# A Mamba layer and a window attention layer on four images: one pipeline over all images per layer, in place of both layers image by image

## The chip, the cores and the metric

The kernel runs on one core of one Trainium2 chip. The metric is the time of one execution in microseconds (us), measured on the device. The engines are PE (matmuls), DVE (VectorE), ACT (ScalarE), POOL (GpSimd) and SP, whose queue issues the DMA transfers.

## The reference, cut to what matters

The input x is 4 images of 384 channels and 64 x 64 points, in fp32. Two layers follow, each with a residual, each on x normalised in groups of 12 channels over a whole image. (The residuals and group norms are not in this cut. `bn_stats`, below, is the DVE instruction that gathers means and variances for them.)

```python
# layer 0, a state space layer: 768 inner channels, 16 states, 4096 points in sequence
xn = layernorm(xs) * ln_w + ln_b
xb, z = split(xn @ in_proj_w.T)
xc = silu(causal_conv4(xb) + conv_b)
dt, Bm, Cm = split(xc @ x_proj_w.T)            # 24 + 16 + 16
dt = softplus(dt @ dt_w.T + dt_b)
h  = exp(dt * A) * h + (dt * xc) * Bm          # point after point
y  = (sum over states of h * Cm) + xc * D
out = (y * silu(z)) @ out_proj_w.T
# layer 1: attention with 12 heads, each point with a 7 x 7 window and a relative bias
```

The group norm is why a layer can't start on an image before it has seen the whole image: its statistics come first.

## The kernel before: the parts that matter here

The sequence of one image is cut into 16 steps of 256 points. For each of 6 channel blocks and each of 4 groups of states, ACT makes `da = exp(dt*A)`, POOL makes `db = dtx*B`, DVE runs four scans (`hp` and `hs`, two each), DVE and POOL multiply by C, and PE adds up the states and turns the result. That is one unit; a step has 24 units and 48 slots, two for each unit. All other work of a step (projections, convolution, a burst of Silu with its table loads, softplus, normalisation, output projection) is put by hand into numbered slots between the scans:

```python
def scan(d, g, h, db, y, ahead):
    ...
    for half, to in ((0, hp), (1, hs)):
        da = ps_a.tile([P, 2, T], F32, tag="da", name="da")       # 2 PSUM banks
        ... # two exponentials on ACT, two scans on DVE
        ahead()                                                   # emits the work of the next slot
# work of a step, by slot
at(26, by_group); at(27, lambda: mean("xn", "mu")); ...           # normalisation of the step after next
pair(("c", p), 9 + 3 * p, ...); at(12 + 3 * p, conv_out)          # convolution on PE, copied out by ACT
at(27, burst)                                                     # six Silu between two table loads
softplus(q, 31 + 3 * q)                                           # q = 0, 1, 2
# output projection of the step before: three tiles on PE, residual on DVE
at(8, lambda: tiles(0, (0,)));  at(9, lambda: tiles(0, (1,)))
at(10, lambda: residual(0, 2))
at(11, lambda: tiles(2, (2,))); at(12, lambda: residual(2, 1))
```

(The calls of `at` are drawn together here.) Most matmul results pass through one pool of three banks of PSUM, the memory into which PE writes. The frame around it handles one image after the other:

```python
bm = ...                           # mask, then 96 small transfers of the relative bias
for b in range(NB):
    ...                            # load x, bn_stats for the group norm
    layer0(b, x1, lambda pool: group_stats(st0, pool, f"a{b}"), st1)
    layer1(b, x1, lambda pool: group_stats(st1, pool, f"b{b}"))
```

## Time and profile before

| | before |
|---|---|
| time | 9843.51 us, median of 3 runs (9839.28 to 9846.54) |
| span of the profiled execution | 9830.4 us |
| step of the state space layer | 104.86 us |
| start, up to the first exponential | 179.4 us |

The page's busy line and three of its rows in 40 slices (a digit is the busy share in tenths):

```profile
PE 7857.1 (80%) x46266; PEld 5693.4 (58%) x46266; DVE 7503.0 (76%) x15348; ACT 5802.9 (59%) x13694; POOL 6099.0 (62%) x5279
...
PE   4787787799777777779968778777997778777899
DVE  3888888655688888865568888885556888888555
...
POOL 2898899400399898830049889893005889889200
```

POOL's row shows the four images: it is busy in the state space layer and idle in attention.

### The profile page before, as it was taken

How to read it: one execution, taken by the hardware profiler on the slowest of the kernel's cores; microseconds unless marked ns; L12 is line 12 of the kernel's file. 1: busy time of each engine (PE TensorE's matmuls, PEld its weight loads, DVE VectorE, ACT ScalarE, POOL GpSimd, SP SyncE). 2: the span in 40 equal slices, each digit the busy share in tenths (PEclk: the TensorE clock that was granted, in tenths of full speed). 3: DMA queues.
4: the chain of work that ended last, by engine and by line, in shares of the span. 5: the costliest groups of instructions: out<-in, count | busy, mean ns of one | idle time of the engine just before them, and what ended most of it. 6: DMA issues, size and time to landing. Idle time of an engine off the chain costs nothing. (4 is left out here: it accounts for less than half of the span.)

```text
span 9830.4 us, 139829 instructions
## 1 busy us (share of the span) xinstructions
PE 7857.1 (80%) x46266; PEld 5693.4 (58%) x46266; DVE 7503.0 (76%) x15348; ACT 5802.9 (59%) x13694; POOL 6099.0 (62%) x5279
## 2 busy tenths in 40 slices
PE   4787787799777777779968778777997778777899
PEld 4666666455566666645556666664555666666455
DVE  3888888655688888865568888885556888888555
ACT  3667667344566666634456766763445766766344
POOL 2898899400399898830049889893005889889200
PEclk9788888799888888789988888888998888887899
DMA  2111111222211111112221111112222111111222
GB/s 82 56 48 42 57 47 40 69 74 68 70 52 45 50 50 45 53 59 77 70 73 45 42 58 45 44 55 71 75 61 72 42 57 47 42 59 42 73 75 61
DMA packets 300170, 563.61 MB, mean 57 GB/s; under 512 B 61196, under 2 KB 183324, under 8 KB 298804
## 3 DMA queue, kind: packets, MB, share of 16 engines
q1 hardware_dynamic: 299444, 554.67, 17.5%
q8 instruction: 365, 5.98, 0.3%
q14 instruction: 361, 2.96, 0.1%
HBM read 452.01 MB, written 84.73 MB: 55 GB/s over the span
## 5 line engine op out<-in xcount | busy, mean ns | idle before, releaser
L96 ACT ACTIVATE da<-dt,nega 128x256 f32<-128x256 f32 x6144 | 2914.2, 477 | 1628.7 <-DVE hs L501 1085.7
L481 POOL TENSOR_TENSOR db<-dtx,B 128x1024 f32<-128x1024 f32 x1536 | 3614.0, 2353 | 30.2
L501 DVE TENSOR_TENSOR_SCAN hp<-da,state,db 128x256 f32<-128x256 f32 x3072 | 2298.6, 748 | 429.5 <-POOL dtx L476 216.2
L501 DVE TENSOR_TENSOR_SCAN hs<-da,state,db 128x256 f32<-128x256 f32 x3072 | 2255.3, 734 | 18.3 <-ACT da L96 15.2
L520 PE MATMUL y<-ident,hv 128*128 128x128 f32 x6144 | 1206.6, 330 | 1145.7 <-DVE hv L507 1144.6
L512 POOL TENSOR_TENSOR hs<-hs,C 128x512 f32<-128x512 f32 x1536 | 1946.5, 1267 | 123.2 <-POOL state L511 0.6
L520 PEld LDWEIGHTS y<-ident,hv 128*128 128x128 f32 x6144 | 859.9, 168 | 1571.6 <-DVE hv L507 1464.6
L96 ACT ACTIVATE sg<-sg,mx 128x308 f32<-128x308 f32 x1536 | 830.3, 542 | 884.0 <-DVE mx L798 883.0
L851 POOL COPY rb<-rsum 128x384 f32<-128x384 f32 x128 | 65.8, 514 | 2052.9 <-DVE rsum L849 1935.2
L520 PE MATMUL y<-ident,hs 128*128 128x128 f32 x6144 | 1165.4, 323 | 141.5 <-POOL hs L512 139.2
L330 PE MATMUL mm_ps<-xn,w_in 128*128 128x256 f32 x4608 | 1118.3, 390 | 14.6 <-DVE xn L306 8.1
L507 DVE TENSOR_TENSOR hv<-hp,C 128x512 f32<-128x512 f32 x1536 | 1043.3, 679 | 0.0
L520 PEld LDWEIGHTS y<-ident,hs 128*128 128x128 f32 x6144 | 899.9, 170 | 206.8 <-POOL hs L512 202.4
L330 PEld LDWEIGHTS mm_ps<-xn,w_in 128*128 128x128 f32 x4608 | 874.9, 198 | 126.4 <-issue 9.9
L798 DVE CUSTOM_DVE_ANT_0 sg<-lg_ps,bias 128x308 f32<-128x308 f32 x1536 | 650.9, 474 | 237.4 <-PE lg_ps L792 226.6
L337 PE MATMUL mm_ps<-xb,dcv 128*128 128x256 f32 x3072 | 723.4, 379 | 0.0
L337 PEld LDWEIGHTS mm_ps<-xb,dcv 128*128 128x128 f32 x3072 | 562.8, 190 | 68.7
L511 POOL COPY state<-hs 128x2 f32<-128x2 f32 x1536 | 286.4, 186 | 500.6 <-DVE hs L501 456.3
L476 POOL TENSOR_TENSOR dtx<-dt,xc 128x256 f32<-128x256 f32 x384 | 279.3, 727 | 465.7 <-DMA B<-bcrows 297.2
L556 PE MATMUL mm_ps<-yg,w_out 128*128 128x256 f32 x2304 | 523.6, 382 | 0.0
L822 DVE COPY ta<-pt_ps 110x512 f32<-110x512 f32 x768 | 495.1, 680 | 25.0 <-PE pt_ps L817 21.7
L556 PEld LDWEIGHTS mm_ps<-yg,w_out 128*128 128x128 f32 x2304 | 437.4, 192 | 57.8
(136 smaller groups left out, 10438.8 us busy)
## 6 DMA issues: line engine op xcount, KB each, us to landing
B<-bcrows SPq DMA_DIRECT2D x256, 512.0 KB
C<-bcrows SPq DMA_DIRECT2D x256, 512.0 KB
vw<-vd SPq DMA_DIRECT2D x1792, 33.0 KB
xr<-x SPq DMA_DIRECT2D x28, 1056.0 KB
vd<-v SPq DMA_DIRECT2D x280, 96.0 KB
xi<-in_x_dram SPq DMA_DIRECT2D x64, 384.0 KB
x<-in_x_dram SPq DMA_DIRECT2D x32, 768.0 KB
x<-xo SPq DMA_DIRECT2D x64, 384.0 KB
```

Of the source, the lines that this page charges most:

```text
L96: ins = nc.scalar.activation(o, i, func, **kw)
L330: nc.tensor.matmul(pb[:, k, :], w_in[:, j, m * P : (m + 1) * P], xn[:, j, :], start=(j == 0), stop=(j == NJ - 1),)
L337: nc.tensor.matmul(pb[:, k, :], dcv[:, d, c, :], xb[:, d, c : c + T], start=(c == 0), stop=(c == KC - 1),)
L481: nc.gpsimd.tensor_tensor(db, h["dtx"].unsqueeze(1).broadcast_to([P, NG, T]), h["bc"][g][0], ALU.mult)
L501: nc.vector.tensor_tensor_scan(to[:, k, :], da[:, k, :], db[:, 2 * half + k, :], state[:, d, n + k : n + k + 1], ALU.mult, ALU.add,)
L507: nc.vector.tensor_tensor(hv, hp, ct[:, 0:2, :], ALU.mult)
L511: nc.gpsimd.tensor_copy(state[:, d, n : n + 2], hs[:, :, T - 1])
L512: nc.gpsimd.tensor_tensor(hs, hs, ct[:, 2:4, :], ALU.mult)
L520: nc.tensor.matmul(y[:, half, :], t[:, k, half * P : (half + 1) * P], ident, is_transpose=True, start=(first and half == 0), stop=(last an ...
L556: nc.tensor.matmul(h["po"][:, m - first, :], w_out[:, d, m * P : (m + 1) * P], h["yg"][d], start=(d == 0), stop=(d == ND - 1),)
L798: nc.vector.tensor_tensor_reduce(sg[:, hh, :], lg[:, :NK], bias[:, 4 * m + hh, :], -1.0, BIG, ALU.add, ALU.min, mx[:, hh : hh + 1],)
L822: nc.vector.tensor_copy(t[: KN[0], :, :].rearrange("p a q -> p (a q)"), pt[: KN[0], :])
```

## The change

Its intent: pay the edges between stages once and not four times. The state space layer runs through all four images as one pipeline of 64 steps, then attention runs through all 32 stripes. The statistics of the next image are taken inside the steps. The first image's loads of x come first of all, and the 96 bias transfers are put into the steps. The slots inside a step are also moved. The core of the diff:

```diff
-    for b in range(NB):
-        ...
-        layer0(b, x1, lambda pool: group_stats(st0, pool, f"a{b}"), st1)
-        layer1(b, x1, lambda pool: group_stats(st1, pool, f"b{b}"))
+    layer0(x1s, mvs)
+    layer1(x1s, mvs)
...
+            def next_batch(b, at):
...
+                for n in range(NJ * NXT):
+                    t, j = divmod(n, NJ)
+                    at(24 * n + 17, lambda t=t, j=j: load(t, j))
+                    at(24 * n + 29, lambda t=t, j=j: nc.vector.bn_stats(st[:, j, t, :], h["x"]))
...
-                at(26, by_group)
+                at(30, by_group)
-                at(34, lambda: with_row("var", ALU.mult))
+                at(38, lambda: with_row("var", ALU.mult))
...
-                    pair(("c", p), 9 + 3 * p, lambda pb, k, d=d: conv(pb, k, d + k))
-                    at(12 + 3 * p, conv_out)
+                    pair(("c", p), 11 + 3 * p, lambda pb, k, d=d: conv(pb, k, d + k))
+                    at(14 + 3 * p, conv_out)
-                at(27, burst)
+                at(29, burst)
-                    softplus(q, 31 + 3 * q)
+                    softplus(q, 33 + 3 * q)
...
-                            state[:, d, n + k : n + k + 1], ALU.mult, ALU.add,
+                            state[:, d, n + k : n + k + 1] if I % NCHUNK else 0.0,
+                            ALU.mult, ALU.add,
...
-                at(10, lambda: residual(0, 2))
-                at(11, lambda: tiles(2, (2,)))
-                at(12, lambda: residual(2, 1))
+                at(10, lambda: tiles(2, (2,)))
+                at(12, lambda: residual(0, 2))
+                at(13, lambda: residual(2, 1))
...
-                    turn(i, d, h, slot_of(i), (d + 1) * (SLOTS // ND) + 5)
+                    turn(I, d, h, slot_of(I), (d + 1) * (SLOTS // ND) + 4)
```

## The prediction

> **What bounds the kernel now.** I read the page first, then a table of busy time by stage, the first and last record of some tiles, and one step of the pipeline engine by engine.
>
> The page gives a span of 9830.4 us in which no engine is busy above 80%. Its rows in 40 slices repeat four times, so I looked at one batch by stage:
>
> ```profile
> core 0: us, PE busy (x) PEld busy (x) DVE busy (x) ACT busy (x) POOL busy (x), PEclk, DMA share, GB/s
> 0.00:179.00 179.00, 70.14 (x291) 58.85 (x292) 34.07 (x80) 31.18 (x64) 9.76 (x21) 0.98 0.35 107
> 179.00:1839.00 1660.00, 1288.60 (x6307) 1031.56 (x6305) 1474.20 (x2640) 1117.66 (x2436) 1496.45 (x1259) 0.82 0.14 46
> 1839.00:1909.00 70.00, 49.66 (x161) 27.91 (x159) 11.48 (x27) 4.18 (x9) 3.02 (x8) 0.88 0.39 121
> 1909.00:2508.00 599.00, 558.80 (x4791) 314.19 (x4790) 357.26 (x1110) 295.95 (x910) 19.68 (x46) 1.00 0.24 70
> 2508.00:2613.00 105.00, 63.59 (x294) 45.70 (x293) 30.46 (x55) 32.61 (x71) 4.09 (x4) 0.81 0.32 112
> ```
>
> The stages are: start, 16 state space steps, a turn to attention, attention, a turn to the next batch. The steps keep DVE and POOL near 90%; attention keeps PE at 93%; in both turns and the start everything waits. The first exponentials (tile da) start at 179.4, 2613.2, 5047.4 and 7480.1, so the batches are alike.
>
> One step takes 104.85 us: POOL's product dtx for the first channel block recurs at that distance.
>
> ```profile
> 589.89 0.73 POOL L476 TENSOR_TENSOR dtx<-dt,xc 128x256 f32<-128x256 f32 x1
> ...
> 694.74 0.73 POOL L476 TENSOR_TENSOR dtx<-dt,xc 128x256 f32<-128x256 f32 x1
> ```
>
> POOL alone would need 15.96 us per block, 95.9 for six with one small copy. DVE's starts in that step give 3.38 us for a unit of four scans, 24 x 3.38 = 81.2, and 11.8 for the rest (dt 6.1, gates 1.9, normalisation 1.7, statistics 1.05, residual 0.95): 93.0. The other 11.9 us are DVE's waits. It almost never waits for POOL's product db (0.3 us a step), so DVE's queue with its waits sets the step. The large ones:
>
> ```profile
> 616.55 0.69 DVE L564 TENSOR_TENSOR xo<-mm_ps,xi 128x512 f32<-128x512 f32 x1 [1.93 <-PE mm_ps L556]
> ...
> 623.47 0.42 DVE L564 TENSOR_TENSOR xo<-mm_ps,xi 128x256 f32<-128x256 f32 x1 [2.83 <-PE mm_ps L556]
> ...
> 656.34 1.55 DVE L501 TENSOR_TENSOR_SCAN hp<-da,state,db 128x256 f32<-128x256 f32 x2 [3.88 <-POOL dtx L476]
> ```
>
> The last is named POOL, but ACT was away from the exponentials in the burst of Silu, from 649.42 to 655.26:
>
> ```profile
> 649.42 1.28 ACT L96 ACT_TABLE_LOAD   x1
> 650.72 1.67 ACT L96 ACTIVATE xc<-xc 128x512 f32<-128x512 f32 x3
> 652.29 1.65 ACT L96 ACTIVATE sz<-sz 128x512 f32<-128x512 f32 x3
> 653.97 1.28 ACT L100 ACT_TABLE_LOAD   x1
> 655.26 1.89 ACT L96 ACTIVATE da<-dt,nega 128x256 f32<-128x256 f32 x4
> ```
>
> **What the Trainium skill says.** "PSUM — Partial Sum Buffer", Engine vs sequencer instructions: the queues of ScalarE, VectorE and GpSimd are strictly first in, first out, and matmuls complete in program order. The trace agrees: the residual's 1.93 and 2.83 us stop scans that were ready. So the place of an instruction in its queue is what this change trades in. "ScalarE: Activation LUTs", What ACT_TABLE_LOAD costs: about 1283 ns a load plus a drain of 1380. The loads are 1.28 us here; no drain shows, as the next activation starts 0.02 us later. "SBUF — State Buffer", SBUF: two separate sides: transfers don't slow an engine's SBUF access. I count the new loads in the steps as free, with DMA at a share of 0.14 there; no single line of before tests it. "Perfetto Trace Analysis", Optimization Strategy, advises interleaving regimes; this change does the opposite, grouping equal ones, and gains only by having fewer edges.
>
> **The change part by part.**
>
> *Start.* The 96 bias transfers (62 us of issue, 30.2 to 92.1) leave it; batch 0's statistics come first. From the first x load to the first group matmul took 22.9 us (92.16 to 115.04), now over by 24. The small vector lnb landed at 15.1; behind eight x loads that took 14.3 to issue it lands at 29.4. The 72 + 18 folding matmuls take 15.5 + 4.0: 49. From the first mean matmul (121.89) to 179.4 were 57.5. First exponential: 107, 72 earlier. In the built program's order the scheduler puts the bias transfers into step 0, before the second step's B and C loads; 62 us fit, since those loads must wait for the last block anyway.
>
> *Steps.* Before: 15 x 104.85 + 86.9 (the last step prepares nothing) = 1659.6 a batch. After: 63 s + 86.9, where s is the new step.
> - The residuals move to slots 12 and 13, the third output tile to 10, so the 4.76 us of waits go. But conv now follows all three tiles on PE: from slot 8, 7.8 us of tiles, 3.5 of conv, 1.7 of y sums, 0.65 of turning, 13.6. PE starts this about 1.5 us ahead of DVE, ACT then needs 1.9 for two copies and two exponentials, so the scan of slot 15 waits some 3 us. In total this place moves from 16.0 to 14.1 us after slot 8, and a later wait of 0.71 goes: -2.7.
> - xn's activations (1.48 us) move behind the burst. The gap around the burst, 4.93 + 0.22, becomes 4.5, but the next exponential comes 1.0 late: up to +0.35.
> - With these shifts the second dt projection (slot 36) finds the three PSUM banks taken; the built program makes it wait for the gate of slot 38. Projection 1.1 to 2.1, four activations 1.45, exponentials 0.95: the scan after slot 38 waits 0.9 to 1.9. Before it 1.2 in place of the 1.0 now. Net about +1.7.
> - Next batch's bn_stats: two a step in 12 of 16 steps of three batches, 0.64 us each; one falls into the burst's gap, one counts: +0.64 x 36/64 = +0.36.
>
> The sum is 104.85 - 2.7 + 0.35 + 1.7 + 0.36 = 104.6. I choose s = 104.0, as two terms are upper ends: 63 x 104.0 + 86.9 = 6638.9. Three chains of group statistics inside steps, some 2 us of small DVE work each: 6.
>
> *Turn to attention, once.* 70.3 (last scan 1839.0 to first score 1909.3). All four group chains now stand before the first projection, with one PSUM bank: three more x 6.3 (1852.4 to 1858.7) = 18.9; the wait of 1.4 for xr goes: 88.
>
> *Attention.* Scores of the eight stripes start at distances of 72.6, 77.6, 79.5 four times, 73.7, and the last, without a next projection, takes 57. At an inner edge the last stripe now projects the next batch's first: PE work 33.5 us in place of a normal stripe's 26.4, which costs 22.5 there; I take 32, so 89. Batch 0: 541.9 + 89; two batches 6 x 79.5 + 73.7 + 89 = 639.7 each; the last 607.7; tail 20.7: 2538.7.
>
> Sum: 107 + 6638.9 + 6 + 88 + 2538.7 = 9378.6 in the trace; the runs' median lies 13.1 above it (9843.51 - 9830.4): 9392.
> Against before (9830.4): start -72; three turns to a batch -315; three turns to attention -211, the one left +18; projections inside attention +32 x 3 = 96, fuller first stripes +26; prepared last steps +18 x 3 = 54, shorter steps -54; group chains +6. That is -452, by the other way round.
>
> **The rivals.**
> (a) The step improves to POOL's floor. For: without the residual waits DVE needs about 100. Against: conv on PE comes at once behind them. s = 99.5 gives 9109.
> (b) The step worsens: the slot 38 wait and the bn_stats count fully and conv is as late as the residual was. s = 107 gives 9581. For: each is a wait in a strict queue. Against: the slots look deliberately set.
> (c) The steps don't move: s = 104.85 gives 9446; only the edges pay.
> (d) The bias transfers clog the queue that also issues B and C: step 0 longer by 20 to 50 us, once.
>
> **Range and chances.** s from 101.5 to 106.3 is -158 to +145 us; start and attention are good to some 30. Range 9230 to 9545. The edges alone give over 4%, so faster by over 2% fails only with s above 108 (9647 is the 2% line): 0.96; within 2% 0.03; slower 0.01.
>
> **What would show it right or wrong.** First exponential near 107; dtx of the first block every 104 us, 101.5 to 106.3; no wait of xo on the output matmuls, but one of the scan near slot 15 and one after slot 38; first scores about 88 after the last scan; score stripes of 79.5, the edge ones near 89; no stretch with all engines idle between batches. I am wrong if steps with bn_stats differ from those without by over 2 us, if the step falls under 100, or if edge stripes exceed 110.

## More of the kernel before

Inside the steps of the first image, this is what DVE waited for (total, number of times, longest), over some 11.5 steps:

```profile
DVE xo L564 <- PE mm_ps L556: 57.0, 24, 2.8
DVE hp L501 <- POOL dtx L476: 42.6, 11, 3.9
DVE hp L501 <- ACT da L96: 15.7, 22, 1.0
```

The first line is the residual that waits for the output projection, the second the gap of the burst, the third mostly the first scan of slot 34.

## The result, and the profile after

The changed kernel takes 9437.55 us (median of 4 runs, 9435.81 to 9438.56); the kernel before in the same rounds took 9841.40. The ratio is 0.9589, 95% interval 0.9572 to 0.9605. Ratios here are the mean time of one kernel's fast runs over that of the other's in the same rounds, so they are not quite the ratio of the medians quoted. The prediction, 9392 us, is 46 us too low, and its range holds the result.

The page after, the same rows as above:

```profile
PE 7804.9 (83%) x46266; PEld 5722.8 (61%) x46266; DVE 7485.8 (79%) x15348; ACT 5773.9 (61%) x13694; POOL 6104.2 (65%) x5271
...
PE   7877887788777877787788777877789999999999
DVE  6888988898889888988898888888755555555555
...
POOL 5888988898989898988889989998700000000000
```

Each engine's busy time is the same to within 1%; the rows no longer repeat, and the dips between stages are gone. The table of busy time by stage, with the edges that the trace of after gives:

```profile
core 0: us, PE busy (x) PEld busy (x) DVE busy (x) ACT busy (x) POOL busy (x), PEclk, DMA share, GB/s
0.00:109.60 109.60, 69.93 (x290) 58.30 (x291) 33.89 (x80) 31.42 (x64) 7.62 (x18) 0.96 0.47 157
109.60:6796.00 6686.40, 5293.41 (x25961) 4299.21 (x25960) 5969.68 (x10719) 4532.23 (x9930) 6009.78 (x5052) 0.82 0.16 51
6796.00:6886.00 90.00, 66.38 (x237) 41.15 (x236) 14.84 (x48) 5.81 (x16) 2.67 (x5) 0.76 0.30 95
6886.00:9410.00 2524.00, 2356.64 (x19644) 1314.28 (x19643) 1457.87 (x4480) 1198.10 (x3668) 83.58 (x196) 1.00 0.26 75
```

There is one start, one stretch of steps, one turn and one stretch of attention. The last scan ends at 6796.1, the first score starts at 6885.2. Set beside the prediction's sum:

| term | predicted | measured | difference |
|---|---|---|---|
| start, to the first exponential | 107 | 109.6 | +2.6 |
| 64 steps, with the group chains | 6644.9 | 6686.5 | +41.6 |
| turn to attention | 88 | 89.1 | +1.1 |
| attention | 2538.7 | 2551.2 | +12.5 |
| from the trace to the runs' median | 13.1 | 1.15 | -11.9 |
| sum | 9391.7 | 9437.55 | +45.9 |

A step still takes about what it took. POOL's product dtx of the first block in the last image, where no statistics are taken any more, again recurs at nearly the old distance, 104.61 us:

```profile
5657.19 0.73 POOL L545 TENSOR_TENSOR dtx<-dt,xc 128x256 f32<-128x256 f32 x1
...
5761.80 0.74 POOL L545 TENSOR_TENSOR dtx<-dt,xc 128x256 f32<-128x256 f32 x1
```

Over many steps, from first scan to first scan, the mean is 105.07 us where the next image's bn_stats run (27 steps, the third to the eleventh of three images) and 104.41 us where they don't (11 steps of the last image); before it was 104.86. What DVE waits for in some 11.5 steps of the last image:

```profile
DVE hs L570 <- ACT da L96: 68.6, 47, 3.1
DVE hp L570 <- POOL state L581: 43.2, 12, 3.6
DVE hp L570 <- ACT da L96: 4.6, 7, 1.1
```

The waits of the residual are gone from the list (57.0 before). In their place the second scans of a unit wait for exponentials, 68.6 us, where before it was 2.6. The wait named POOL is the burst's gap again. Two moments of one step make up most of the 68.6. The first is slot 15:

```profile
5679.81 5.35 PE L628 MATMUL mm_ps<-yg,w_out 128*128 128x256 f32 x24
...
5685.87 2.76 PE L628 MATMUL mm_ps<-yg,w_out 128*128 128x256 f32 x12
5688.46 1.89 PE L400 MATMUL mm_ps<-xb,dcv 128*128 128x256 f32 x8
...
5691.72 1.89 PE L400 MATMUL mm_ps<-xb,dcv 128*128 128x256 f32 x8
...
5693.65 0.84 ACT L96 ACTIVATE xc<-mm_ps,cvb 128x256 f32<-128x256 f32 x2 [4.93 <-PE mm_ps L400]
...
5695.40 0.75 DVE L570 TENSOR_TENSOR_SCAN hs<-da,state,db 128x256 f32<-128x256 f32 x1 [3.05 <-ACT da L96]
```

PE does three output tiles (lines with w_out), then the two halves of the convolution. ACT stands 4.93 us in front of its copy of the convolution, with the exponentials of the next scan behind it in the queue, and the scan pays 3.05. The second moment is slot 38:

```profile
5744.11 0.41 DVE L617 TENSOR_TENSOR yg<-mm_ps,sz 128x256 f32<-128x256 f32 x1
...
5744.57 2.07 PE L500 MATMUL mm_ps<-xd,w_dt 24*128 24x256 f32 x4 [5.16 <-DVE yg L617]
...
5746.68 0.48 ACT L96 ACTIVATE spe<-mm_ps,dtb 128x256 f32<-128x256 f32 x1 [4.12 <-PE mm_ps L500]
...
5749.16 0.75 DVE L570 TENSOR_TENSOR_SCAN hs<-da,state,db 128x256 f32<-128x256 f32 x1 [1.73 <-ACT da L96]
```

PE has waited 5.16 us for a PSUM bank that the gate yg (DVE's product of a block's result with its silu(z)) frees; ACT waits for PE, and the scan waits 1.73 for ACT. Both waits are those that the prediction had worked out.

Attention ran as before, but for the stripe that also projects the next image's first stripe. Here it is (first line, up to the next stripe's first score) beside the very last stripe, which projects nothing, from its first score to its last:

```profile
7426.90:7520.80 93.90, 87.74 (x685) 48.85 (x683) 48.66 (x146) 39.82 (x119) 3.25 (x7) 1.00 0.24 67
...
9358.50:9415.00 56.50, 54.39 (x521) 31.92 (x523) 39.52 (x127) 33.59 (x106) 1.53 (x3) 1.00 0.20 59
```

### The profile page after: what moved, and what is told of

Same layout as the page of the kernel before. It is cut to its first block, busy times and chain, and to the rows that moved or that the text cites.

```text
span 9436.4 us, 139560 instructions
## 1 busy us (share of the span) xinstructions
PE 7804.9 (83%) x46266; PEld 5722.8 (61%) x46266; DVE 7485.8 (79%) x15348; ACT 5773.9 (61%) x13694; POOL 6104.2 (65%) x5271
## 4 chain that ended last, share of the span: by engine, by line
PE 36%; DVE 28%; ACT 16%; POOL 10%; issue 9%; DMA 0%; SPq 0%; DVEq 0%; ACTq 0%; POOLq 0%
DVE hp L570 9%; DVE hs L570 8%; POOL db L550 5%; DVE hv L577 5%; PE mm_ps L628 5%; ACT da L96 4%; POOL hs L582 4%; PE y L590 3%; ACT sg L96 3%; PE mm_ps L393 3%; PE lg_ps L887 3%; PE mm_ps L969 3%; PE mm_ps L792 3%; PE mm_ps L855 3%; PE pt_ps L912 2%
## 5 line engine op out<-in xcount | busy, mean ns | idle before, releaser
L570 DVE TENSOR_TENSOR_SCAN hs<-da,state,db 128x256 f32<-128x256 f32 x2880 | 2118.6, 736 | 347.8 <-ACT da L96 347.8
L570 DVE TENSOR_TENSOR_SCAN hp<-da,state,db 128x256 f32<-128x256 f32 x2880 | 2153.8, 748 | 303.0 <-POOL state L581 192.9
L393 PE MATMUL mm_ps<-xn,w_in 128*128 128x256 f32 x4608 | 1163.9, 404 | 2.0 <-DVE xn L369 2.0
L393 PEld LDWEIGHTS mm_ps<-xn,w_in 128*128 128x128 f32 x4608 | 925.3, 207 | 133.3 <-issue 3.4
L500 PE MATMUL mm_ps<-xd,w_dt 24*128 24x256 f32 x768 | 335.4, 577 | 289.9 <-DVE yg L617 287.0
L927 ACT COPY tb<-pt_ps 88x512 f32<-88x512 f32 x384 | 223.1, 581 | 392.2 <-PE pt_ps L923 392.2
```

The costliest lines, as they stand in the source:

```text
L393: nc.tensor.matmul(pb[:, k, :], w_in[:, j, m * P : (m + 1) * P], xn[:, j, :], start=(j == 0), stop=(j == NJ - 1),)
L500: nc.tensor.matmul(t["pb"][:, k, :], w_dt[:, (2 * q + k) * P : (2 * q + k + 1) * P], h["xd"][:DTR, :], start=True, stop=True,)
L570: nc.vector.tensor_tensor_scan(to[:, k, :], da[:, k, :], db[:, 2 * half + k, :], state[:, d, n + k : n + k + 1] if I % NCHUNK else 0.0, AL ...
```

## The experiments

Twelve kernels ran. Each is the changed kernel with the edit shown, unless another is named. The table gathers the steps, read from the traces in the way just told.

| kernel | median, us | ratio to before | step with bn_stats | without |
|---|---|---|---|---|
| changed kernel | 9437.55 | 0.9589 | 105.07 | 104.41 |
| e1_old_slots | 9447.74 | 0.9604 | 104.99 | 104.91 |
| e2_dt_later | 9318.86 | 0.9473 | 103.14 | 102.55 |
| e3_conv_out | 9383.69 | 0.9539 | 104.11 | 103.56 |
| e4_both | 9284.61 | 0.9438 | 102.54 | 101.96 |
| e5_bias_first | 9450.79 | 0.9606 | 104.93 | 104.37 |
| e6_conv_17 | 9224.63 | 0.9376 | 101.36 | 101.34 |
| e7_bn_gap | 9413.34 | 0.9567 | 104.43 | 104.35 |
| e8_best | 9158.41 | 0.9309 | 100.30 | 100.29 |
| e9_norm_in_steps | 9424.15 | 0.9577 | 105.09 | 104.44 |
| e10_all | 9151.01 | 0.9300 | 100.36 | 100.36 |
| e11_half_hs (wrong result) | 9111.01 | 0.9259 | 99.57 | 99.57 |
| e12_before_x_first | 9785.04 | 0.9945 | none | as before |

The medians of the kernel before in the four sets of rounds lay between 9837.09 and 9841.40 us, so a difference between kernels of different sets is sure to some 4 us only. (e1_old_slots lies 10 us above the changed kernel by the medians, and 15 by the ratios.)

### The edges alone: e1_old_slots

```diff
-                at(30, by_group)
+                at(26, by_group)
...                                   # every slot inside the step as in the kernel before
-                at(14 + 3 * p, conv_out)
+                at(12 + 3 * p, conv_out)
```

> One pipeline as in the changed kernel, but the slots inside a step as in the kernel before (output tiles, residuals, convolution, burst, softplus, normalisation, turning). My theory: the new slots gain 2.6 us a step between slots 8 and 18 and give 2.0 back in the second half, so they are worth only 0.45 us a step (104.86 before, 104.41 now without bn_stats), 28 us in 63 steps; moreover the second bn_stats no longer falls into the gap of the burst, up to 0.64 x 36 = 23. Expected 9465 to 9490 us. Rival: the slots are what makes the long pipeline pay, and without them a step takes 106.5 or more: 9545 us or more.

It took 9447.74 us, 10 more than the changed kernel and 390 less than before. The 390 us are not the edges between images alone: this kernel also has the new start, with its first exponential at 111.6 us in place of 179.4, and e12_before_x_first, below, gains 55 us by loading x first and nothing else. The rest, some 335 us if the two add up, is one pipeline in place of four. The rival, that the new slots carry the long pipeline, falls. My own figure was too high as well. The step without bn_stats returned to 104.91 as expected, but the steps with them took only 104.99. The trace shows why: with the old slots one bn_stats stands just ahead of the residual's wait, which shrinks from 1.93 to 1.32 us, and the other ahead of the wait of slot 34, which shrinks from 1.03 to 0.52. In the changed kernel the wait of the residual is gone, and so is the place to hide in. The new slots save 0.50 us in a step without bn_stats and lose 0.08 in one with them.

### The wait at slot 38: e2_dt_later

```diff
-                    softplus(q, 33 + 3 * q)
+                    softplus(q, (33, 39, 42)[q])
```

> The changed kernel with the second and third dt projection and softplus three slots later (slots 39 and 42 in place of 36 and 39), so that their PSUM bank is free when PE comes to them. My theory: the scan after slot 38 then loses its wait of 1.66 us a step and gains none: 63 x 1.7 = 105 us, so about 9332 us. Rival: ScalarE's work is the same and only comes later, so the wait moves to the scans of slots 40 to 47: 9437 us, within 20.

It took 9318.86 us, 119 less than the changed kernel. The scan after slot 38 no longer waits, nor does one of 0.44 us in slot 4; only 0.5 came up elsewhere (slot 43), and the step lost 1.86 to 1.93 us. The rival falls. No bank was added: the projection is merely asked for after slot 38 has freed the three.

### The wait at slot 15: e3_conv_out, and both: e4_both

```diff
-                    at(14 + 3 * p, conv_out)
+                    at(16 + 2 * p, conv_out)
```

> The changed kernel with ScalarE's three copies of the convolution out of PSUM at slots 16, 18 and 20 in place of 14, 17 and 20; the matmuls stay. My theory: ScalarE waits in slot 14 for a convolution that PE can begin only after the three output tiles, and the scan of slot 15 pays 3.06 us a step for it; this wait goes or falls under 0.5: 63 x 2.6 to 3.06 = 164 to 193 us, so 9245 to 9275 us. Rival: the wait is PE's or POOL's in truth and comes back at the next unit or at the burst: 9437 us, within 20.

It took 9383.69 us: 54 less, where I had expected 164 to 193 and the rival none. The wait at slot 15 went in full, but the scans of slots 19 and 21 now wait 0.6 and 1.7 us: PE is busy without a gap until the last convolution, and ACT's copies at slots 18 and 20 are again early. I had looked at the first copy alone.

> Both moves of the two kernels before together. If the two waits are independent parts of VectorE's queue, the gains add: 9437 - 105 - 180 = about 9150 us, a step of about 100.1 us. Rival: GpSimd's own work (95.9 us of it a step, a floor of 99.5 with its waits) takes over and only two thirds arrive: 9220 to 9260 us.

9284.61 us, a gain of 153 over the changed kernel; the two gains alone sum to 173 (118.7 + 53.9). The expected 9150 failed with e3's figure. The rival's range, 9220 to 9260, is missed too. It named POOL, but the trace shows the waits of slots 19 and 21 behind the convolution still in place, so this run doesn't speak for it.

### The same one slot later: e6_conv_17

```diff
-                    at(14 + 3 * p, conv_out)
+                    at(17 + 2 * p, conv_out)
-                    softplus(q, 33 + 3 * q)
+                    softplus(q, (33, 39, 42)[q])
```

> As the kernel with both moves, but ScalarE copies the convolutions out one slot later still, at 17, 19 and 21. In that kernel PE was busy without a gap up to the end of each convolution, and the scans of slots 19 and 21 still waited 0.6 and 1.7 us. My theory: these waits go too, 2.0 to 2.3 us a step: 9284 - 126 to 145 = 9140 to 9160 us. Rival: at a step of 99.7 us GpSimd (floor of 99.5) is met, VectorE starts to wait for its products db, and less than half arrives: 9210 to 9260 us.

9224.63 us, in the rival's range. The waits behind the convolution fell to 0.24 us and less, but between slots 22 and 28 DVE now waits for POOL's db, up to 1.0 us at a time and 19.4 us in some 12 steps. Of the 2.3 us only 0.62 to 1.18 arrived.

### The next image's statistics: e7_bn_gap

```diff
-                    at(24 * n + 17, lambda t=t, j=j: load(t, j))
-                    at(24 * n + 29, lambda t=t, j=j: nc.vector.bn_stats(st[:, j, t, :], h["x"]))
+                    at(48 * (n // 2) + 17, lambda t=t, j=j: load(t, j))
+                    at(48 * (n // 2) + 29, lambda t=t, j=j: nc.vector.bn_stats(st[:, j, t, :], h[t, j]))
```

(Two tiles for the loads; the tile xo has one buffer in place of two, for space.)

> The changed kernel with both bn_stats of the next batch in slot 29, in the gap of the burst, in place of one in slot 5 and one in slot 29 (same loads and same bytes, two tiles for them). My theory: the cost of the next batch's statistics is VectorE's place alone: 0.66 us in 36 steps, 24 us, so 9413 us, and steps with and without them alike within 0.15 us. Rival: the loads into SBUF or their semaphores slow the step: 9437 us and the difference of 0.66 stays.

9413.34 us, as expected: 24 less, with steps of 104.43 and 104.35. The same bytes are loaded, so neither the loads nor their semaphores cost anything that shows; the price of the statistics was one bn_stats a step in slot 5, where nothing else was being waited for.

### The start: e5_bias_first and e12_before_x_first

```diff
+    with tc.tile_pool(name="fill", bufs=1) as fpool:
+        masked(fpool.tile([P, TX], F32, name="fill"))
+    for qi in range(RB):
+        biased(qi)
...
-            slot_of(0)(1, mask)
-            for qi in range(RB):
-                slot_of(3 + qi)(40, lambda qi=qi: biased(qi))
```

> The changed kernel with the mask and the 96 bias transfers back ahead of the pipeline (behind the weights, before the first step's load of x). My theory: they cost their 62 us of issue there in full, as before, and nothing at the place where the change put them: about 9500 us, first exponential near 172, and the first steps as long as in the changed kernel. Rival: in the changed kernel they also hold up the B and C loads of the first steps, so moving them out gives back 20 to 50 us: 9450 to 9480 us.

It took 9450.79 us, only 13 more. Both texts missed: mine by 49, and the rival's range began where the result fell but for another cause, as the first steps were no shorter overall. The queue of transfers at the start:

```profile
34.73 7.72 SPq L352 DMA_DIRECT2D xi<-in_x_dram  x2
52.13 62.09 SPq L236 DMA_DIRECT2D bm<-in_rel_bias_dram  x96
114.33 0.52 SPq L483 DMA_DIRECT2D bcrows<-xd  x1
```

The 96 transfers still take 62 us to issue, but x and the weights have been issued by then, and the engines spend this time on statistics, folding and the first normalisation, which need nothing from the queue. Only B and C wait behind them: the first exponential comes at 112.8, the first scan at 128.2 in place of 111.8. So what made the start shorter was that x comes first. The counter-test is the kernel before with its x loads moved to the top and nothing else:

```diff
+    st0_0 = small.tile([P, NJ, NXT, 6], F32, tag="st0", name="st0_0")
+    ...                               # loads of x[0] and their bn_stats, ahead of the weights
-            for t in range(NXT):
+            for t in range(NXT if b else 0):
```

> The kernel before, with one thing altered: the loads of the first batch for its statistics stand ahead of the weights and the 96 bias transfers. The run with the bias transfers back at the start lost only 13 us, not 62. My theory now: what the start gains is that x comes first; the 62 us of issue then lie beside the statistics, folding and normalisation and cost some 15. Expected: first exponential near 115, first scan near 130, 9837 - 50 = about 9787 us. Rival: the transfers must leave the start for the gain: 9820 to 9840 us.

9785.04 us, 55 less than before, as expected (first exponential at 108.8, first scan at 120.3).

### The group statistics at the turn: e9_norm_in_steps

```diff
+            def attention_norm(b, at):
+                gm1s.append(small.tile([P, NJ, 2], F32, tag="gm1", name=f"gm_b{b}", bufs=NB))
+                for n, part in enumerate(group_stats(mvs[b], gm1s[b], ps, f"b{b}")):
+                    at(50 + 3 * n, part)
...
+            for b in range(NB - 1):
+                attention_norm(b, slot_of((b + 1) * NCHUNK))
```

> The changed kernel with the attention layer's group statistics of the first three batches computed inside the steps (each in the second step of the following batch) and only the last batch's at the turn. The turn took 89.1 us from the last scan to the first score. My theory: three chains of 6.3 us leave it (18.9), and three chains in the steps cost 1.5 to 2.8 each, as those of the next batch do: a turn of about 70 us and 9437 - 13 = 9424 us. Rival: the chains at the turn lie beside the first loads of the attention layer, so the turn keeps 80 us or more and the total is 9437 to 9443 us.

9424.15 us: 13.4 less, as expected. The turn fell from 89.1 to 69.9 us (6802.6 to 6872.5). The last scan ended 6.5 us later; 2.3 of that came in the start (first scan at 114.2 in place of 111.8), and the steps took 4.2 more. So the turn's term in the prediction, three chains in a row with nothing beside them, holds.

### All together: e8_best and e10_all

e8_best takes e6 and e7 together and moves two lines more:

```diff
-                at(37, root)
-                at(38, lambda: with_row("var", ALU.mult))
+                at(38, root)
+                at(40, lambda: with_row("var", ALU.mult))
```

> All moves together: later dt projections, convolutions copied at 17, 19, 21, both bn_stats in the burst's gap, and the root of the variance at slot 38 with the product at 40 in place of 37 and 38 (the scan of slot 37 waited 0.75 us while ScalarE waited for the matmul of the variance). If VectorE's queue still sets the step: the kernel with convolutions at 17, less 24 and less 47, about 9075 us. Rival, GpSimd's floor of 99.5 us: not under 9130 us, with VectorE waiting for db.

9158.41 us, correct, 279 less than the changed kernel. It misses the first figure by 83 and is what the rival allows: not under 9130, with DVE waiting for db. The 9075 was counted from the 9140 to 9160 that was expected of e6; from e6's measured 9224.63 the same 24 and 47 give 9154, but that agreement is luck. In e6 the steps with and without bn_stats were already alike (101.36 and 101.34), so the gap for bn_stats had nothing left to give, and the step lost 1.06 us in both kinds. All of it lies in slots 37 to 43, where the two moved lines stand. The wait that the text names, 0.76 us in slot 37, stayed: ACT is then busy with the softplus. What went are those of 0.15 in slot 38 and 0.49 in slot 43, with time around them. No run has the two lines alone.

DVE's waits in some 12 steps of it:

```profile
DVE hp L570 <- issue: 38.3, 12, 3.2
DVE hp L570 <- POOL db L550: 18.0, 47, 0.8
DVE hs L570 <- ACT da L96: 14.8, 25, 0.8
```

The first line is the burst's gap (the trace names no releaser), the second is POOL, which now runs 15 of a step's 24 units back to back: three blocks take 15.98 to 16.01 us each from dtx to dtx, the fourth 16.43 (the text of e11 below says four).

> All moves of the run before (9158 us) together with the group statistics inside the steps. If the two are independent: 9158 - 13 = 9145 us. If the chains cost more where GpSimd leaves no slack in the step: 9150 to 9160 us.

9151.01 us, correct, ratio 0.9300, the fastest correct kernel. The chains are worth 7 us here and not 13, as the second text allowed: the steps grew by 8.8 us over those of e8_best, against 4.2 in e9_norm_in_steps. That POOL is the reason is not shown.

### Is POOL the bound now? e11_half_hs

```diff
-                    nc.gpsimd.tensor_tensor(hs, hs, ct[:, 2:4, :], ALU.mult)
+                    nc.gpsimd.tensor_tensor(hs[:, 0:1, :], hs[:, 0:1, :], ct[:, 2:3, :], ALU.mult)
```

> Wrong result on purpose: the kernel of 9158 us in which GpSimd multiplies only one of the two states of hs by C, 24 x 0.6 = some 15 us less of its work a step; nothing changes for VectorE, ScalarE and PE. My theory: at a step of 100.3 us GpSimd's work now sets four of the six blocks (15.99 us each, its own floor), so VectorE's waits for db, about 0.3 to 0.8 at a time, go and the step falls to 97.5 to 99 us: 8980 to 9075 us. Rival: VectorE's queue still sets the step and GpSimd only keeps pace: 9158 us, within 15.

9111.01 us, with a wrong result as intended: 47 less, a step of 99.57. My text expected at least 83, the rival at most 15, so both missed. With 12.9 us less work for POOL in a step (96.06 to 83.17) the step lost 0.72 us, while the gap of the burst grew from 3.19 to 3.57. So POOL accounts for some 0.7 us of e8's step, and what is left is DVE's own queue with the gap that ACT's table loads and Silu leave in it. What a shorter burst would give was not tried.

## Why the prediction was right, and where its terms were off

**Direction and source: right.** The edges pay, together with the start. e1_old_slots has the two without the new slots and takes 390 of the 404 us, of which e12_before_x_first explains 55 by x alone. Rival (c), only the edges pay, gave 9446 and was nearer than my own figure.

**The step: the terms were right, the choice was wrong.** The failed step is "I choose s = 104.0, as two terms are upper ends". The sum of the terms was 104.6. In the prediction's own accounting the trace gives (6686.5 - 86.9 - 6) / 63 = 104.66. The 0.6 that I took off, times 63, is 38 of the 46 us that were missing. The terms, one by one, in steps without bn_stats:

- Output tiles and convolution, slots 8 to 17: 23.94 us before, 21.50 now, so -2.44; predicted -2.7. The wait near slot 15 is 3.06; predicted some 3.
- The rest of the step: 80.92 before, 82.91 now, +1.99; predicted 0.35 + 1.7 = 2.05. The scan after slot 38 waits 1.62 to 1.69; predicted 0.9 to 1.9. The waits just ahead of it (slots 37 and 38) are 0.91; predicted 1.2, in place of the 1.0 of before. The gap of the burst with the scan of slot 31 behind it went from 3.87 to 4.06; predicted up to +0.35. I had called two terms upper ends; together they were the size.
- bn_stats: 105.07 - 104.41 = 0.66 in a step that has two of them; predicted 0.64, "one falls into the burst's gap, one counts". e7_bn_gap shows this mechanism.

Not foreseen: the first step of an image begins its scans with the constant 0 in place of a stored state. These scans take 684 ns on average and not 742, and the first steps of the second to fourth image take 101.67, 101.58 and 101.68 us. None of them holds the bn_stats of slot 5, so they are to be set beside 104.41: together 8.3 us less (2.74 + 2.83 + 2.73). By their mean times the scans save 5.6 us a step, but these steps also have waits that others lack (0.9 us of yg for PE, 0.6 of a scan for db). No run alters the start value alone, so what it is worth stays open. Without the shorter steps the mean would have been a little further above the sum.

**Start: the number was right, its reason only in part.** 109.6 against 107. But "the 96 bias transfers (62 us of issue) leave it" is not what saved the time: e5_bias_first puts them back and loses 13, and e12_before_x_first gains 55 with them in place. Rival (d), the transfers clog step 0, falls: in the changed kernel that step took 100.6 us, less than those after it.

**Turn: right.** 89.1 against 88; e9_norm_in_steps confirms the three chains in it, which follow each other at 5.8 us (predicted 6.3).

**Attention: one term mis-sized.** The inner edge stripe took 93.9 us and not 89. The projection's PE work was as predicted, 87.7 - 54.4 = 33.3 us, but I let some of it hide and added 32; in fact the whole of it and 4 us of waits came on top of the last stripe's 57 (93.9 - 57 = 36.9). Three edges, less a stripe behind each that took 78.6 and not 79.5, give 3 x 4.9 - 3 x 0.9 = 12.0 of the 12.5. The normal stripes kept 79.5.

**Trace to median: mis-sized, and it helped.** I added 13.1 us, the distance of before's trace from its median. Most of that was chance: the profiled execution of before, 9832.11 us, was faster than all four timed ones. A span lies 1.7 to 1.9 us under its own execution's time. This error of -11.9 hid a fifth of the others (57.8).

None of the signs named as refuting came: steps with bn_stats differ by 0.66 us, no step fell under 100 but the last but one (99.6), for which less was left to prepare, and the edge stripes stayed under 110 (93.9).

## What to carry to other kernels

Where stages of different limits alternate, count the edges first: running all images through one stage before the next paid some 335 us here, and loading x ahead of all else 55, while a retuning of the slots that looked careful paid 10 to 15, as it traded one engine's place in a queue for another's. A sum of worked-out waits should be left as it stands; an allowance "because some terms are upper ends" was the largest error here. And before work is moved into a pipeline, look for a wait in which it can stand: the same bn_stats cost 0.66, 0.08 and 0.08 us a step in three places, and moving two pieces of work later by a few slots, behind the release of the PSUM bank or the matmul that they need, gave more than the whole retuning had.

## What the Trainium skill lacked or had wrong

- "ScalarE: Activation LUTs", What ACT_TABLE_LOAD costs: the load of about 1283 ns agrees (1.28 us), but the drain of about 1380 ns after a switch is not seen in the burst, where the next activation starts 0.02 us after the load's end (650.72 after 649.42 + 1.28).
- No page that I found says what a stored start costs VectorE's scan. Here a scan of 128x256 with a stored state as its start took 742 ns on average, and 684 with a constant.
- "Perfetto Trace Analysis", Optimization Strategy: its advice to interleave regimes doesn't name the cost of each change of regime; grouping equal ones took some 335 us off (the 390 of e1_old_slots less the 55 of e12_before_x_first). Its remark that a gap which keeps recurring can mean too little PSUM for the next tile fits slot 38, but the cure was the order and not the space: the three banks stayed three, and asking for one three slots later gave 119 us (e2_dt_later).
